# Queries' input loaded by row groups and turned by VectorE in place of TensorE, with each group's first scores ahead of its products, in a prompt-token cross-attention kernel

## Chip, core and metric

The kernel runs on one core of one Trainium2 chip. The metric is the device time of one execution in microseconds (us). The engines are named as in the profile: PE is TensorE (matrix products and transposes), PEld its loading of weights, DVE is VectorE, ACT is ScalarE, POOL is GpSimd, and SP is SyncE, which here only issues DMAs. The time before is 429.61 us, the median of three runs (429.59 to 430.12).

## What is computed

Cross-attention with 20 heads of width 16 over 371 text tokens, plus a second attention over four prompt tokens whose logits get a cosine term. The batch has 8 elements of 112 queries with 320 channels; the context has 375 rows of 512, the last four being the prompt tokens. All is fp32. The reference, cut to what matters:

```python
B, S, C = hidden_states.shape                      # 8, 112, 320
text_ehs, ip_ehs = ehs[:, :-4], ehs[:, -4:]        # 371 and 4 rows of 512
q = heads(hidden_states @ W_q)                     # 20 heads of 16
k_t, v_t = heads(text_ehs @ W_k), heads(text_ehs @ W_v)
probs_t = softmax(einsum('bhsd,bhtd->bhst', q, k_t) * attn_scale)
text_out = einsum('bhst,bhtd->bhsd', probs_t, v_t)
k_ip, v_ip = heads(ip_ehs @ W_k_ip), heads(ip_ehs @ W_v_ip)
qsem = l2norm(einsum('bhst,bte->bhse', probs_t, text_ehs))
sem = einsum('bhse,bne->bhsn', qsem, l2norm(ip_ehs))
fused = einsum('bhsd,bhnd->bhsn', q, k_ip) * attn_scale + 0.5 * sem
probs_ip = softmax(fused) * spatial_mask[None, None, :, None]
out = (text_out + einsum('bhsn,bhnd->bhsd', probs_ip, v_ip)) @ W_out + b_out + x
```

The kernel never forms qsem. Its norm is a quadratic form of the probabilities in the Gram matrix of the context, and its product with the prompt tokens is a product of the probabilities with a small matrix.

## The kernel before

**Steps.** The work runs in 40 steps (b, g): eight batch elements, five groups of four heads each. A step's main work on PE are the *products* (`multiplied`, L748): the turned probabilities times `u`, a matrix that holds the upper blocks of the Gram matrix, the values and the prompt columns. They go over 12 blocks of 32 text tokens, and in each block over the group's four heads, which sit in four 32-row groups of PE and sum in four PSUM banks (pool `ps_qd`, tag "qd", four buffers, one bank for each head). At the step's end ACT copies the values' columns out of each bank (`value_sums`, L761), and DVE multiplies the rest with the probabilities and reduces it (`reduced`, L794, tile `junk`, sum `ss`). After its reduction a bank is free for the next step's products.

**The way from scores to products.** The *scores* (L686, tile `ps_s`, pool `ps_sc`, two buffers) of step n + 2 are made during step n: those of heads 2 and 3 behind the first block of the products, those of heads 0 and 1 behind the seventh. For each, DVE takes the maximum (L709, `nmx`), ACT the exponential (L712, `p`) and copies the four prompt scores (L714, `ipl`), and SP issues a DMA that brings the probabilities into a row-grouped layout (L721, `xg`). After the third block of the products, DVE turns the next step's `xg` into `xgT` (L729, a 32x32 block transpose).

**Work between the steps.** `between(b, g)` issues, behind the products of each step, what the next element needs: the Gram matrix at g = 0 and with it the turn of a later context on DVE (L404), the values at g = 1 and 2 (L578), the keys at g = 2, 3 and 4 (L544; the last third is put together by PE transposes of `k3`, L535), the output of the element before (`finish`: transposes of `attn` into `ps_a`, L950, copied by ACT to `aT`, L954; the output product `ps_o`, L962). These use the pool `ps_mm` (tag "mm", two buffers), or a buffer of the scores' pool where `bank(..., spare=True)` asks for it.

**Queries.** `project_queries` prepares the queries of one or two elements: element 0 in the prologue, the pair (1, 2) over step (0,1) and what follows, (3, 4) from step (1,3) on, (5, 6) from (3,3), 7 from (5,3). PE transposes x in three pieces of 128, 128 and 64 channels (L333, `ps_x`), ACT copies each to `xT` (L336), and three products with W_q (L344, `ps_q`) follow at later places, whose results DVE masks into `qm` (L353). For a pair, the first product stands at g = 4 of the first element, the second and third at g = 3 and 4 of the next.

**Order.** The order on PE, SP and DVE is that of the code, and in the prologue and from the main loop on that of ACT too. Waits come only from the data, the buffers of the pools, and SP's DMA semaphores: there are eight in turn, so that a DMA of SP waits until the eighth before it has landed. All input loads of the prologue go through SP in one row.

Of the kernel before, what the change touches and what calls it, by code (L numbers as in the profile page):

```python
# [20 lines left out]
def kernel(  # L21
# [149 lines left out]
    make_identity(nc, ident)  # L171
    nc.gpsimd.memset(wq_sb[REST:, FULL, :], 0.0)

# [141 lines left out]
    def project_queries(bs):  # L315
        n = len(bs)
        end = bs[0] == B - 1
        xT = work.tile([P, NC, 2 * S], F32, tag="xT", name=f"xT_{bs[0]}", bufs=1)
        qm = work.tile([P, NC, 2, 2 * S], F32, tag="qm", name=f"qm_{bs[0]}", bufs=2)

        qT = const.tile([P, NC, S], F32, tag="qT", name="qT") if bs[0] == 0 else None
        for j, b in enumerate(bs):
            queries[b] = (qT, qm, j)
        nc.gpsimd.memset(xT[REST:, FULL, :], 0.0)
        for i in range(NC):
            cn = min(P, C - i * P)
            if bs[0] == 0:

                ps = ps_qd.tile([P, 512], F32, tag="qd", name=f"ps_x_0_{i}")
            else:  # L330
                ps = bank(f"ps_x_{bs[0]}_{i}", spare=i > 0)
            for j, b in enumerate(bs):
                nc.tensor.transpose(  # L333
                    ps[:cn, j * S : (j + 1) * S], x_sb[:, b, i * P : i * P + cn], ident[:S, :S]
                )
            nc.scalar.copy(xT[:cn, i, : n * S], ps[:cn, : n * S])  # L336
            yield
        for i in range(NC):
# [4 lines left out]
            for j in range(NC):  # L343
                nc.tensor.matmul(  # L344
                    ps[:, : n * S],
                    wq_sb[:, j, i * P : (i + 1) * P],
                    xT[:, j, : n * S],
                    start=(j == 0),
                    stop=(j == NC - 1),
                )  # L350
# [174 lines left out]
    def keys(b):  # L525
# [409 lines left out]
    def prompt_sums_and_projection(b, s, eng, part, n, h0, i0, i1, w, attn, ah):  # L935
# [11 lines left out]

        ps = bank(f"ps_a_{b}_{h0}", spare=True)
        for i in range(i0, i1):
# [129 lines left out]
    def between(b, g):  # L1079
# [16 lines left out]
        if g == 1:  # L1096
            if new:
                run(("v", nb), lambda: values(nb), 1 if b == 0 else 2)
            if b == 0:
                run(("pp",), prompt_projections)  # L1100
            for bs in first if b == 0 else ():
                run(("q", bs[0]), lambda: project_queries(bs), 3)
        if g == 2 and new:
            run(("v", nb), None)
            run(("k", nb), lambda: keys(nb))
            for bs in first if b == 0 else ():
                run(("q", bs[0]), None)
        if g == 2 and b > 0 and new:
            run(("f", b - 1), None, 2)
        if g == 3:  # L1110
            if new:
                run(("k", nb), None, 1)
            if b > 0 and new:
                run(("f", b - 1), None)
            for bs in first if b > 0 else ():
                run(("q", bs[0]), lambda: project_queries(bs), 3)
            if b == 0:
                run(("t", b), lambda: prompt_logits(b))
            for bs in rest:
                run(("q", bs[0]), None)  # L1120
        if g < NT and nb + 1 < B:
            run(("c", nb + 1), lambda: transposed_context(nb + 1))
        if g == 4:
            if b > 0 and new:
                run(("f", b - 1), None, 2)
            if nb < B - 1:
                run(("k", nb), None, 1)
            for bs in (first if b > 0 else []) + (rest if b < B - 2 else []):
                run(("q", bs[0]), None)

    prompts = normalised_prompts()
# [9 lines left out]
    next(context)  # L1141
    order_values()
    drain(products)
    nc.scalar.preload_act_table(AF.Exp)
    gram_to_groups(0, range(QN - 1))
    run(("v", 0), lambda: values(0))
    run(("q", 0), lambda: project_queries(pairs[0]), 3)
    gram_to_groups(0, (QN - 1,), nc.scalar)
# [9 lines left out]
    for a in range(GROUP):  # L1158
        scores(0, 0, a, early=True)
        probabilities(0, 0, a)  # L1160
    drain(transposed_context(1))
    run(("q", 0), None)
    run(("k", 0), None)
    for a in range(GROUP):
        scores(0, 1, a, early=True)
        probabilities(0, 1, a)
    load_embed(nc.sync, wkip_sb, w_k_ip)
    load_embed(nc.sync, wvip_sb, w_v_ip)
# [11 lines left out]
    def load_rest(n):  # L1180

        if n == 0:
            load_x(1, 3)
        elif n == 2:
# [217 lines left out]
```

## Time and profile before

| what | value |
|---|---|
| runs: median (lowest to highest) | 429.61 us (429.59 to 430.12) |
| the profiled execution | 429.75 us |
| its span in the trace | 428.0 us |
| instructions in the trace | 13975 |
| mean granted clock of PE | 0.999 of full |

The span is the time from the first to the last recorded instruction; 1.75 us of the execution lie around it. The timelines give start and duration in us, then the engine, line, operation and tiles; instructions of one kind that follow each other are put together with their count, and in brackets stands an idle time before them with what ended it. A group's row gives its busy time in all, the mean of one in ns, and its idle time before.

### The profile page before, as it was taken

To read this page: it belongs to the slowest core of one execution; us is meant where nothing else is said; L and a number is where in the kernel's file an instruction comes from. 1 tells how busy PE (TensorE), PEld (TensorE's weight loads), DVE (VectorE), ACT (ScalarE), POOL (GpSimd) and SP (SyncE) were. 2 spreads that over 40 slices of the span, in tenths; PEclk is the share of its full clock that TensorE was granted. 3 is DMA by queue.
4 is the path that set the end of the run, shared out by engine and by line. 5 is a ranking of instruction groups with operands and counts; after the bars stand their busy time and mean duration, and the time that the engine had idled before them with its cause. 6 is when DMAs were issued, how large, how long until landed. Compare 5 with 4: busy or idle time off the path is not lost.

```text
span 428.0 us, 13975 instructions
## 1 busy us (share of the span) xinstructions
PE 419.5 (98%) x5521; PEld 330.3 (77%) x5521; DVE 327.8 (77%) x672; ACT 189.7 (44%) x659; POOL 111.1 (26%) x275
## 2 busy tenths in 40 slices
PE   8999999989999999999999999999999999999995
PEld 8867768878777877789777977788777887687993
DVE  5038569787887879788797878887788977889873
ACT  2344342346334353345435363334634363446773
POOL 5310101112060212411152121511133120515550
PEclk9999999999999999999999999999999999999999
DMA  8776665687645956476646956468556536564200
GB/s 239 199 192 211 140 169 157 160 200 149 166 123 138 207 152 179 123 162 150 168 121 160 189 124 170 127 153 175 141 166 153 145 96 173 156 159 121 65 2 27
DMA packets 57630, 64.26 MB, mean 150 GB/s; under 512 B 18448, under 2 KB 51592, under 8 KB 57566
## 3 DMA queue, kind: packets, MB, share of 16 engines
q1 hardware_dynamic: 56934, 62.42, 58.2%
q8 instruction: 43, 0.70, 0.8%
q10 hardware_dynamic: 632, 0.96, 0.7%
q14 instruction: 21, 0.17, 0.1%
HBM read 18.67 MB, written 5.32 MB: 56 GB/s over the span
## 4 chain that ended last, share of the span: by engine, by line
PE 90%; DVE 3%; ACT 3%; DMA 1%; issue 1%; POOL 0%; DVEq 0%; ACTq 0%
PE ps_qd L748 43%; PE ps_v L578 15%; PE ps_k L544 10%; PE ps_g L502 7%; PE ps_s L686 5%; PE ps_q L344 3%; PE ps_o L962 2%; PE ps_g L458 1%; DVE junk L794 1%; ACT shared L787 1%; DMA xg<-p 1%; DVE nmx L709 1%; DMA ct<-in_ctx_dram 1%; PE ps_k L560 1%; PE ps_c L417 1%
## 5 line engine op out<-in xcount | busy, mean ns | idle before, releaser
L748 PE MATMUL ps_qd<-u,xgT 32*112 32x168 f32 (+11 forms) x3840 | 221.7, 353 | 0.3 <-POOL u L655 0.3
L748 PEld LDWEIGHTS ps_qd<-u,xgT 32*112 32x112 f32 x3840 | 189.0, 172 | 33.7 <-issue 10.4
L729 DVE STREAM_TRANSPOSE xgT<-xg 128x1536 f32<-128x1536 f32 (+1 forms) x45 | 119.3, 2672 | 6.7 <-DMA xg<-p 6.7
L712 ACT ACTIVATE p<-ps_s,nmx 112x371 f32<-112x371 f32 x156 | 84.8, 582 | 74.8 <-DVE nmx L709 63.5
L709 DVE TENSOR_REDUCE nmx<-ps_s 112x1 f32<-112x371 f32 x160 | 77.5, 529 | 42.2 <-PE ps_s L686 41.3
L794 DVE CUSTOM_DVE_ANT_0 junk<-ps_qd,p 112x371 f32<-112x371 f32 x146 | 79.2, 542 | 17.4 <-PE ps_qd L748 1.4
L686 PE MATMUL ps_s<-kT,qm 32*112 32x375 f32 (+1 forms) x320 | 65.5, 484 | 0.1
L655 POOL COPY u<-vr 128x64 f32<-128x64 f32 x120 | 25.9, 238 | 152.4 <-PE ps_qd L748 100.9
L578 PE MATMUL ps_v<-wv_sb,ctxT 128*128 128x384 f32 (+1 forms) x192 | 63.6, 480 | 0.0
L578 PEld LDWEIGHTS ps_v<-wv_sb,ctxT 128*128 128x128 f32 x192 | 35.2, 190 | 19.7
L544 PE MATMUL ps_k<-ctxT,wk_sb 128*128 128x371 f32 x136 | 46.3, 483 | 0.2 <-DVE ctxT L425 0.2
L761 ACT COPY pvs<-ps_qd 112x21 f32<-112x21 f32 x151 | 16.3, 190 | 62.3 <-PE ps_qd L748 61.9
L544 PEld LDWEIGHTS ps_k<-ctxT,wk_sb 128*128 128x128 f32 x136 | 24.9, 190 | 15.2 <-POOL ct L138 0.5
L502 PE MATMUL ps_g<-ctxT 128*32 128x375 f32 (+11 forms) x672 | 30.4, 333 | 0.0
L686 PEld LDWEIGHTS ps_s<-kT,qm 32*112 32x112 f32 x320 | 26.7, 170 | 4.8 <-ACT kT L551 2.0
L502 PEld LDWEIGHTS ps_g<-ctxT 128*32 128x32 f32 x672 | 27.7, 110 | 2.0
L714 ACT COPY ipl<-ps_s 112x4 f32<-112x4 f32 x140 | 23.5, 168 | 0.0
L353 DVE TENSOR_SCALAR qm<-ps_q,emask 128x224 f32<-128x224 f32 (+1 forms) x25 | 9.0, 394 | 17.1 <-PE ps_q L344 17.1
L585 ACT COPY vext<-ps_v 128x384 f32<-128x384 f32 (+1 forms) x24 | 11.3, 469 | 22.4 <-PE ps_v L578 22.3
L404 DVE STREAM_TRANSPOSE ctxT<-ct 128x512 f32<-128x512 f32 x18 | 19.9, 1108 | 1.6 <-DMA ct<-in_ctx_dram 1.6
L475 POOL TENSOR_TENSOR ug<-ug,half 128x128 f32<-128x128 f32 (+1 forms) x24 | 10.5, 450 | 31.9 <-ACT ug L474 31.9
L937 POOL TENSOR_TENSOR wv<-vip,w 112x1280 f32<-112x1280 f32 x6 | 14.8, 2466 | 14.2 <-DVE w L877 14.2
(171 smaller groups left out, 323.8 us busy)
## 6 DMA issues: line engine op xcount, KB each, us to landing
xg<-p SPq DMA_DIRECT2D x156, 162.3 KB
u<-ug SPq DMA_DIRECT2D x124, 99.0 KB
ct<-in_ctx_dram SPq DMA_DIRECT2D x24, 176.0 KB
vr<-vd SPq DMA_DIRECT2D x32, 120.0 KB
vip<-vipd SPq DMA_DIRECT2D x6, 560.0 KB
vd<-vext SPq DMA_DIRECT2D x7, 320.0 KB
vd<-vext SPq DMA_DIRECT2D x7, 160.0 KB
out_dram<-ob SPq DMA_DIRECT2D x8, 140.0 KB
```

Of the source, the lines that this page charges most:

```text
L404: nc.vector.transpose(ctxT[:, :, c * P : (c + 1) * P].rearrange("p e (j i) -> p j e i", i=RG), ct[:, some, :].rearrange("p j (k e) -> p j ...
L502: nc.tensor.matmul(ps[c][q * RG : (q + 1) * RG, j * RG - c * P : T - c * P], ctxT[:, e, j * RG : (j + 1) * RG], ctxT[:, e, j * RG : T], st ...
L544: nc.tensor.matmul(ps[:, :TT], wk_sb[:, e, i * P : (i + 1) * P], s["ctxT"][:, e, :TT], start=(e == 0), stop=(e == NE - 1),)
L578: nc.tensor.matmul(ps[:, :w], ctxT[:, e, c * P : (c + 1) * P], wv_sb[:, e, :w], start=(e == 0), stop=(e == NE - 1),)
L655: nc.gpsimd.tensor_copy(v, dealt(b, c, s["vr"][:, c * QN : (c + 1) * QN, g, :]))
L686: nc.tensor.matmul(ps[:S, :w], qm[a * RG : (a + 1) * RG, i, r, j * S : (j + 1) * S], s["kT"][a * RG : (a + 1) * RG, i, :w], start=True, st ...
L709: nc.vector.tensor_reduce(nmx, ps[:S, :TT], AX.X, ALU.max, negate=True)
L712: nc.scalar.activation(s["p", g][:, a, :], ps[:S, :TT], AF.Exp, bias=nmx)
L714: nc.scalar.copy(s["ipl"][:, groups[g][a], :], ps[:S, TT:T])
L729: nc.vector.transpose(xT[:, j : j + n].rearrange("p j (k q) -> p q j k", q=QN), xg[:, :, j * RG : (j + n) * RG].rearrange("p q (j k) -> p ...
L748: nc.tensor.matmul(banks[a][:S, j * RG : UW], xT[a * RG : (a + 1) * RG, j, :S], region(b, c)[a * RG : (a + 1) * RG, q, j * RG - c * P :], ...
L794: nc.vector.tensor_tensor_reduce(out=junk, in0=ps[:S, :TT], in1=s["p", g][:, a, :], scale=1.0, scalar=0.0, op0=ALU.mult, op1=ALU.add, accu ...
```

## The change

x is loaded a second time, into `xr_sb`: the 320 channels in four blocks of 80, each block in 32 partitions that hold 28 queries, and four such groups of queries side by side on the free axis. That takes four DMAs for an element, each with runs of 80 floats. One DVE instruction per element (a 32x32 block transpose, L349 in the new file) turns it straight into `xT`; PE's transposes, ACT's copies and POOL's clearing of `xT` go. The channels come out in another order, so W_q is loaded with its rows in the same order (`load_blocks`, eight DMAs instead of two). The query products read `xT` in four runs of 28 columns.

The other parts: the turns stand in `between` at g = 0 and 1 of element 0 and at g = 2 and 3 of elements 1, 3, 5 (at 5 only g = 2); the loads for them at g = 0 and 2 of these elements and in the prologue. The scores of heads 2 and 3 come ahead of the products instead of behind their first block. At g = 2 the keys come ahead of the values. The last keys of element 1 use a buffer of `ps_mm`, and so do all `ps_a`. The prompt logits of element 0 move from g = 3 to g = 4. The plain load of x for element 0 leaves the prologue.

```diff
+    xr_sb = const.tile([P, 2, QN, NC * RG], F32, tag="xr_sb", name="xr_sb")
+    nc.vector.memset(xr_sb[:, 0], 0.0)
     wq_sb = const.tile([P, NC, CP], F32, tag="wq_sb", name="wq_sb")
+    nc.vector.memset(wq_sb[:, FULL, :], 0.0)
...
+    XB = C // QN
+    XR = XB - 2 * RG
+
+    def load_blocks(eng, t, w):
+
+        for a in range(QN):
+            eng.dma_start(
+                t[a * RG : (a + 1) * RG, :2, :C],
+                w[a * XB : a * XB + 2 * RG, :].rearrange("(e k) f -> k e f", k=RG),
+            )
+        for a in range(QN):
+            eng.dma_start(t[a * RG : a * RG + XR, 2, :C], w[a * XB + 2 * RG : (a + 1) * XB, :])
+
+    def load_x_blocks(b, j):
+
+        for a in range(QN):
+            nc.sync.dma_start(
+                xr_sb[a * RG : a * RG + S // QN, j, :, :XB],
+                x[b, :, a * XB : (a + 1) * XB].rearrange("(q i) f -> i q f", q=QN),
+            )
...
-    nc.sync.dma_start(x_sb[:, 0, :], x[0])
-    load_channels(nc.sync, wq_sb, w_q)
+    load_x_blocks(0, 0)
+    load_blocks(nc.sync, wq_sb, w_q)
     load_embed(nc.sync, wk_sb, w_k)
...
-    nc.gpsimd.memset(wq_sb[REST:, FULL, :], 0.0)
+    nc.gpsimd.memset(xr_sb[:, 1], 0.0)
...
-        xT = work.tile([P, NC, 2 * S], F32, tag="xT", name=f"xT_{bs[0]}", bufs=1)
+        xT = work.tile([P, NC, 2, QN, RG], F32, tag="xT", name=f"xT_{bs[0]}", bufs=1)
...
-        nc.gpsimd.memset(xT[REST:, FULL, :], 0.0)
-        for i in range(NC):
-            cn = min(P, C - i * P)
-            if bs[0] == 0:
-
-                ps = ps_qd.tile([P, 512], F32, tag="qd", name=f"ps_x_0_{i}")
-            else:
-                ps = bank(f"ps_x_{bs[0]}_{i}", spare=i > 0)
-            for j, b in enumerate(bs):
-                nc.tensor.transpose(
-                    ps[:cn, j * S : (j + 1) * S], x_sb[:, b, i * P : i * P + cn], ident[:S, :S]
-                )
-            nc.scalar.copy(xT[:cn, i, : n * S], ps[:cn, : n * S])
+            nc.vector.transpose(
+                xT[:, :, j].rearrange("p e q i -> p q e i"),
+                xr_sb[:, j].rearrange("p q (e k) -> p q e k", k=RG),
+            )
             yield
...
-                    xT[:, j, : n * S],
+                    xT[:, j, :n, :, : S // QN],
...
-            ps = bank(f"ps_k_{b}_{i}", spare=0 < b < B - 1 and i == FULL)
+            ps = bank(f"ps_k_{b}_{i}", spare=1 < b < B - 1 and i == FULL)
...
-        ps = bank(f"ps_a_{b}_{h0}", spare=True)
+        ps = bank(f"ps_a_{b}_{h0}")
...
         if g == 2 and new:
+            run(("k", nb), lambda: keys(nb))
             run(("v", nb), None)
-            run(("k", nb), lambda: keys(nb))
...
-            for bs in first if b > 0 else ():
-                run(("q", bs[0]), lambda: project_queries(bs), 3)
...
+        for bs in first:
+            if g in ((0, 1) if b == 0 else (2, 3)[: len(bs)]):
+                run(("q", bs[0]), lambda: project_queries(bs))
...
+        if g in (0, 2) and b + 2 in (3, 5, 7) and b + 2 + g // 2 < B:
+            load_x_blocks(b + 2 + g // 2, g // 2)
...
         now, more, then = ahead(n)
+        for c, a in now:
+            scores(*c, a)
+            probabilities(*c, a)
         for j, _ in enumerate(multiplied(b, g)):
             if j == 0:
-                for c, a in now:
-                    scores(*c, a)
-                    probabilities(*c, a)
```

Three places show what this does to the order. First PE behind the products of step (1,3): the keys, the output's transposes, and then the next step (1,4). `ps_x` are the transposes of x, `ps_qd_4_0` to `_3` the four banks of the products, `ps_s_1_2` and `ps_s_1_3` scores of heads 2 and 3. Before:

```order
L544 MATMUL ps_k_1_1678<-ctxT_617,wk_sb 128x371 x4
L950 MATMUL ps_a_0_1684<-ident,attn_145 128x112 x3
L333 MATMUL ps_x_0_1693<-ident,x_sb 128x112 x2
L333 MATMUL ps_x_1_1697<-ident,x_sb 128x112 x2
L333 MATMUL ps_x_2_1701<-ident,x_sb 64x112 x2
L748 MATMUL ps_qd_4_0_1705<-u_360,xgT_4_1603 112x392
L748 MATMUL ps_qd_4_1_1706<-u_360,xgT_4_1603 112x392
L748 MATMUL ps_qd_4_2_1707<-u_360,xgT_4_1603 112x392
L748 MATMUL ps_qd_4_3_1708<-u_360,xgT_4_1603 112x392
L686 MATMUL ps_s_1_2_1713<-kT_618,qm_750 112x375
L686 MATMUL ps_s_1_3_1721<-kT_618,qm_750 112x375
```

The same place now:

```order
L560 MATMUL ps_k_1_1689<-ctxT_628,wk_sb 128x371 x4
L966 MATMUL ps_a_0_1695<-ident,attn_157 128x112 x3
L702 MATMUL ps_s_1_2_1702<-kT_629,qm_638 112x375
L702 MATMUL ps_s_1_3_1710<-kT_629,qm_638 112x375
L764 MATMUL ps_qd_4_0_1717<-u_367,xgT_4_1614 112x392
L764 MATMUL ps_qd_4_1_1718<-u_367,xgT_4_1614 112x392
L764 MATMUL ps_qd_4_2_1719<-u_367,xgT_4_1614 112x392
L764 MATMUL ps_qd_4_3_1720<-u_367,xgT_4_1614 112x392
```

The six transposes of x are gone, and the two scores stand ahead of the step's first product instead of behind its fourth. At (2,3) the rows of the keys and of `ps_a` are followed by the second query product, in both kernels:

```order
L560 MATMUL ps_k_1_2373<-ctxT_1304,wk_sb 128x371 x4
L966 MATMUL ps_a_0_2379<-ident,attn_158 128x112 x3
L360 MATMUL ps_q_1_2385<-xT_1579,wq_sb 128x224 x3
L702 MATMUL ps_s_1_2_2391<-kT_1305,qm_1580 112x375
L702 MATMUL ps_s_1_3_2399<-kT_1305,qm_1580 112x375
```

What moved there is the buffer: `ps_k_1` and `ps_a_0` now take the two buffers of `ps_mm` in turn, and `ps_q_1` that of `ps_k_1`; before, `ps_a_0` took one of the scores' pool. The third place is DVE behind the reductions of step (1,2), with the turn of a context (`ctxT`), the maxima for step (1,3)'s scores and the turn of the probabilities for step (1,4). Now:

```order
L420 STREAM_TRANSPOSE ctxT_1304<-ct_1108 128x4x4x32
L349 STREAM_TRANSPOSE xT_1579<-xr_sb 128x4x3x32
L725 TENSOR_REDUCE nmx_0_2_1585<-ps_s_0_2_1583 112x1
L725 TENSOR_REDUCE nmx_0_3_1593<-ps_s_0_3_1591 112x1
L745 STREAM_TRANSPOSE xgT_4_1614<-xg_155 128x4x384
```

The second row is new; before, the maxima (L709) followed the context's turn (L404) directly.

More of the change, by code (lines that the diff above doesn't have):

```diff
@@ L1129, in between @@
                 run(("q", bs[0]), None)
+            if b == 0:
+                run(("t", b), lambda: prompt_logits(b))
     prompts = normalised_prompts()
@@ L1142 @@
     order_values()
+    run(("q", 0), lambda: project_queries(pairs[0]))
     drain(products)
@@ L1146 @@
     run(("v", 0), lambda: values(0))
-    run(("q", 0), lambda: project_queries(pairs[0]), 3)
     gram_to_groups(0, (QN - 1,), nc.scalar)
@@ L1160 @@
         probabilities(0, 0, a)
+    load_x_blocks(1, 0)
     drain(transposed_context(1))
@@ L1166 @@
         probabilities(0, 1, a)
+    load_x_blocks(2, 1)
     load_embed(nc.sync, wkip_sb, w_k_ip)
```

6 lines of the change are left out of this document (1 added, 5 removed).

## Prediction

> **What bounds the kernel now.** I read the page's busy row first, then the granted clock, then the chain of work that ended last.
>
> ```profile
> PE 419.5 (98%) x5521; PEld 330.3 (77%) x5521; DVE 327.8 (77%) x672; ACT 189.7 (44%) x659; POOL 111.1 (26%) x275
> PEclk9999999999999999999999999999999999999999
> PE 90%; DVE 3%; ACT 3%; DMA 1%; issue 1%; POOL 0%; DVEq 0%; ACTq 0%
> ```
>
> PE (TensorE) is busy for 98% of the span at the full granted clock, and nine tenths of the chain is PE. So work taken off PE shortens the kernel by about its own length, unless something else is late at that place. Two engines can be: DVE (77%), which frees the four product banks with its reductions, and ACT (ScalarE, 44%), which frees the others. The profiled execution took 429.75 us (span 428.0); the median of the runs is 429.61, .14 lower. I sum against 429.75.
>
> **Part 1: the transposes that leave PE.** Five groups of queries are prepared: b = 0 in the prologue, then pairs beside step (0,1) and steps (1,3), (3,3), (5,3). From PE's timeline, prologue, (0,1), (1,3) and (5,3):
>
> ```profile
> 16.25 0.45 PE L333 MATMUL ps_x<-ident,x_sb 112*128 112x112 f32 x3
> 16.54 4.49 PE L578 MATMUL ps_v<-wv_sb,ctxT 128*128 128x320 f32 x16
> ...
> 59.89 0.79 PE L333 MATMUL ps_x<-ident,x_sb 112*128 112x112 f32 x6
> 60.62 0.93 PE L748 MATMUL ps_qd<-u,xgT 32*112 32x392 f32 x8
> ...
> 128.70 0.55 PE L333 MATMUL ps_x<-ident,x_sb 112*128 112x112 f32 x4
> 129.47 0.38 PE L333 MATMUL ps_x<-ident,x_sb 112*64 112x112 f32 x2 [0.23 <-ACT aT L954]
> 129.78 1.22 PE L748 MATMUL ps_qd<-u,xgT 32*112 32x392 f32 x10
> 130.55 0.48 PE L686 MATMUL ps_s<-kT,qm 32*112 32x375 f32 x2
> ...
> 326.18 0.35 PE L333 MATMUL ps_x<-ident,x_sb 112*128 112x112 f32 x2
> 327.17 1.22 PE L748 MATMUL ps_qd<-u,xgT 32*112 32x392 f32 x9
> ```
>
> From start to start, PE spends .29 in the prologue (16.25 to 16.54), .73 at (0,1) and 1.08 at (1,3) (128.70 to 129.78, its wait for ACT's aT in it). Step (3,3) has the same instructions as (1,3), so 1.08 too. That is 3.18. At (5,3) .99 stand on PE, but there the chain shows what is late next:
>
> ```profile
> 326.75 3.14 DMA xg<-p
> 329.97 2.14 DVE xgT L729
> ```
>
> The probabilities' turn through a DMA and DVE carries the end there, not PE. PE ahead by .99 gains a part only; I take .4, between 0 and .99.
>
> **Part 2: the stalls that go with them, and the scores moved ahead.** First the one wait that the waits view puts on the copy that is removed, then PE's timeline at (0,2), at the end of (0,4), and at (2,2):
>
> ```profile
> PEld ps_s L686 <- ACT xT L336: 0.7, 1, 0.7
> ```
>
> ```profile
> 61.60 0.79 PE L686 MATMUL ps_s<-kT,qm 32*112 32x371 f32 x2
> ...
> 87.12 0.54 PE L535 MATMUL ps_k<-ident,k 128*128 128x128 f32 x3 [1.08 <-ACT ipl L714]
> 88.74 1.32 PE L748 MATMUL ps_qd<-u,xgT 32*112 32x392 f32 x9
> ...
> 158.97 1.22 PE L748 MATMUL ps_qd<-u,xgT 32*112 32x392 f32 x9
> 159.87 0.63 PE L748 MATMUL ps_qd<-u,xgT 32*112 32x392 f32 x3
> ```
>
> At (0,2) the score starts .98 after the step's first product (60.62 to 61.60), at (1,4) .77 (129.78 to 130.55): .2 lost at least, .7 at most by the wait. I take .5. At (0,4) the keys wait 1.08 for ACT to leave a score bank; the transposes now use another bank, so that wait goes. The products behind them need the fourth product bank, which DVE leaves in its own time, so I count .8, between 0 and 1.08. At (2,2) the tenth product waits for DVE and starts at 159.87, .90 after the first; ten products and the scores behind them normally fill .77, of which the tenth starts at about .48. So .42 goes if scores of about .6 (four, in two pairs) stand ahead and cover it. Nowhere else does the moved score change what PE does: it is the same instruction a place earlier, and it gives DVE its input .77 sooner. Sum of part 2: 1.72.
>
> **Part 3: the turn on DVE.** Eight new transposes of 128x384 (seven of them in steps). The nearest rows are other transposes by the same instruction:
>
> ```profile
> L404 DVE STREAM_TRANSPOSE ctxT<-ct 128x512 f32<-128x512 f32 x18 | 19.9, 1108 | 1.6 <-DMA ct<-in_ctx_dram 1.6
> L729 DVE STREAM_TRANSPOSE xgT<-xg 128x1536 f32<-128x1536 f32 x35 | 104.2, 2978 | 6.7 <-DMA xg<-p 6.7
> ```
>
> (2978 − 1108) / (1536 − 512) = 1.83 ns an element; 1108 − 128 x 1.83 = 874 ns, so .87 us each, 7.0 for eight; between .70 (the slope alone) and 1.11 (no less than for 512). What hides it is DVE's wait for PE's scores, which the waits view totals; DVE's timeline at (1,2) to (1,4) shows where the wait is and where it isn't:
>
> ```profile
> DVE nmx L709 <- PE ps_s L686: 41.3, 35, 3.4
> ```
>
> ```profile
> 120.62 1.11 DVE L404 STREAM_TRANSPOSE ctxT<-ct 128x512 f32<-128x512 f32 x1
> 122.04 0.99 DVE L709 TENSOR_REDUCE nmx<-ps_s 112x1 f32<-112x371 f32 x2 [0.31 <-PE ps_s L686]
> ...
> 128.77 0.55 DVE L794 CUSTOM_DVE_ANT_0 junk<-ps_qd,p 112x371 f32<-112x371 f32 x1
> 131.37 0.99 DVE L709 TENSOR_REDUCE nmx<-ps_s 112x1 f32<-112x371 f32 x2 [2.05 <-PE ps_s L686]
> ```
>
> The turn of g = 3 falls in the 2.05 before 131.37 and is hidden. The turn of g = 2 comes right behind 120.62 and ends at about 122.6, where the maximum started at 122.04: DVE is .5 later for the step, and the fourth bank comes free at about 129.8 instead of 129.3 (128.77 + .55). PE, now at 128.70 where its transposes stood, does its scores (.6) and three products and wants that bank at about 129.5. So some .3 is lost at b = 1 and as much at b = 3; b = 5 has its own term. **.6 off the gain**, between 0 and 1.0.
>
> [...]
>
> **Part 4: a new wait for the queries.** In the changed order the output's transposes (ps_a) take the bank that the second query product used to find free, so that product now takes the bank of the keys just ahead and waits for ACT's copy of them. From PE's and ACT's timelines at (2,3):
>
> ```profile
> 178.03 0.45 PE L950 MATMUL ps_a<-ident,attn 112*128 112x112 f32 x3
> 178.32 1.31 PE L344 MATMUL ps_q<-xT,wq_sb 128*128 128x224 f32 x6
> ```
>
> ```profile
> 178.23 0.47 ACT L551 COPY kT<-ps_k 128x371 f32<-128x371 f32 x1 [1.15 <-PE ps_k L544]
> ```
>
> PE could start the queries at 178.32; ACT is done at 178.23 + .47 = 178.70. That is .4 at each of (2,3), (4,3) and (6,3), with the next step's scores and products queued behind: **1.2 off the gain**, between 0 (if DVE is what the step waits for anyway) and 1.2.
>
> **Part 5: the extra DMAs.** Each load of x by row groups is four DMAs on SP, in the prologue W_q is eight instead of two. From SP's, POOL's, DVE's and PE's timelines of the prologue:
>
> ```profile
> 4.85 1.03 SPq L119 DMA_DIRECT2D wk_sb<-in_L_xattn_W_k_dram  x1
> 9.70 0.29 SPq L155 DMA_DIRECT2D ct<-in_ctx_dram  x1
> 24.92 1.88 SPq L603 DMA_DIRECT2D vr<-vd  x4
> 40.08 5.69 SPq L145 DMA_DIRECT2D ct<-in_ctx_dram  x4
> 45.93 3.55 SPq L721 DMA_DIRECT2D xg<-p  x4
> ```
>
> ```profile
> 16.40 0.40 POOL L1153 COPY wv_sb<-wk_sb 128x256 f32<-128x256 f32 x1
> ```
>
> ```profile
> 52.08 2.97 DVE L729 STREAM_TRANSPOSE xgT<-xg 128x1536 f32<-128x1536 f32 x1
> ```
>
> ```profile
> 21.54 2.76 PE L544 MATMUL ps_k<-ctxT,wk_sb 128*128 128x371 f32 x8
> ```
>
> In the program each of SP's DMAs waits for the eighth before it to have landed. The last ct piece at 9.70 is the eighth after wv_in; now the fourth W_q block is, so it goes at 9.70, four more of .47 (1.88 / 4, pieces of the same run length) follow, and W_k leaves at about 11.9 instead of 4.85. Its transfer takes between 3.1 (the xg row above) and 11.6 (4.85 to its first reader at 16.40), so it lands between 15 and 23.5; PE needs it at 21.25. I take nothing, with up to 2.2 in the range. Later, eight more pieces (3.8 us of SP) stand ahead of the third context's pieces and the xg of 45.93; the first four fall where SP waits for probabilities anyway, the other 1.9 push xg and with it DVE's turn at 52.08. DVE's reductions then end about 60.2, where PE without its transposes wants the first bank at 59.9: **.3 off**, between 0 and 1.0.
>
> The other edits have one answer: keys ahead of values at g = 2, the bank of k at b = 1 (its price is in the .8), prompt_logits at g = 4 and the two DVE memsets at the start are the same work in places where ACT, POOL and SP have over 20% idle; nothing, within .3 either way. Were ACT late, the price would be one copy, .47.
>
> **The sum:** −3.18 − .40 − 1.72 + .6 + 1.2 + .3 = −3.2, so 429.75 − 3.2 = **426.5**. Chance .50.
>
> **The rivals.**
> - **All stalls go** (.16): DVE is .77 earlier from the scores ahead, ACT frees the keys' bank before PE comes. The three costs (2.1) vanish, (5,3) gains its .99, (0,4) its 1.08: 423.5. For it speaks the 41.3 of DVE's waiting; against it that at 122.04 only .31 of it is left.
> - **The gain is given back** (.11): the query products read xT in four runs of 28 columns instead of one row. No row shows such an operand. Their group is
>
> ```profile
> L344 PE MATMUL ps_q<-xT,wq_sb 128*128 128x224 f32 (+1 forms) x90 | 16.8, 323 | 0.1
> ```
>
> if each costs a sixth more, 2.8 of 16.8 come back: 429.3. Nothing in the rows speaks for or against the size; the same columns are read in number.
> - **Slower: the turn isn't hidden** (.10). DVE sets the pace of the odd batches: each of the eight turns then delays the banks by its .87, 7.0 in place of my .6, 432.9. It decides where the fourth bank (129.8) is later than PE by more than what DVE's next wait for scores gives back; 2.05 at 131.37 speaks against it.
> - **Slower: the small loads are slow** (.06). If each of the twelve pieces of x and W_q cost SP what the ct pieces at 40.08 did (5.69 / 4 = 1.42), W_k would be issued at 3.3 + 12 x 1.42 = 20.3 and land, by 3.1 to 11.6, at 23.4 to 31.9: 2 to 10 late, at 6.8 (near the middle) 5.9: 432.4. [...]
> - **Prologue late by 1 to 2** (.07): W_k at the long end of part 5: 428.
>
> **How the numbers follow.** Range 422.5 to 430.0: down to the lower ends of parts 3 to 5 with a little over, up to the case that gives the gain back. About .2% (.86 us) is what a measurement of this kernel can tell from no change. Faster by more: the forecast .50, all stalls .16, the late prologue .07 and .01 of the gain given back, .74; within: .10; slower: .16.
>
> **What would show it.** No transposes or copies of x on PE and ACT; PE's start at (1,4) about 1 us earlier relative to the keys ahead; the wait of ps_qd for DVE's sums at (1,4) and (3,4) near .3; the second query product waiting for ACT's kT by about .4 three times; the new transposes at .87; W_k's first reader before 21. I am wrong if DVE's wait for scores falls by much more than 7 us with PE's wait for DVE rising, if the query products' mean rises, or if PE's first keys start after 22.

## The result, and the profile after

The changed kernel takes 428.32 us (median of 20 runs, 426.54 to 430.84); the kernel before took 429.74 beside it (median of 20, 429.03 to 431.05). The ratio is 0.997, with a 95% interval of 0.9956 to 0.9984: faster, by 1.4 us as the medians stand (.7 to 1.9 by the interval). The forecast was 3.2. The direction held and the time lies in the range, but less than half of the gain came. The profiled execution took 428.22 us at a span of 426.2, so it stands close to the median; 1.53 less than the profiled one of before.

The page's busy row and the chain's engines, after:

```profile
PE 416.0 (98%) x5497; PEld 325.1 (76%) x5497; DVE 331.8 (78%) x682; ACT 185.6 (44%) x644; POOL 109.4 (26%) x270
PE 86%; DMA 4%; DVE 4%; ACT 3%; issue 1%; SPq 1%; ACTq 0%; POOL 0%; DVEq 0%
```

PE has 3.5 us less to do (416.0 against 419.5), which is the transposes that left. The span fell by half of that, and the chain has a new part: DMA went from 1% to 4%. To see where, I take the start of the last product of a step in both timelines:

| last product of step | before, us | after, us | difference |
|---|---|---|---|
| (0,0) | 42.24 | 44.40 | +2.17 |
| (1,0) | 94.62 | 95.85 | +1.23 |
| (1,4) | 134.96 | 135.18 | +.22 |
| (2,2) | 164.60 | 164.21 | −.39 |
| (3,4) | 233.90 | 232.81 | −1.09 |
| (4,4) | 283.21 | 282.72 | −.49 |
| (6,4) | 381.82 | 380.63 | −1.19 |
| of the kernel | 414.51 | 412.68 | −1.83 |

From the end of (0,0) on, the changed kernel gains 4.0 us (2.17 + 1.83), more than forecast. **It loses 2.2 us before its first step has ended.** PE's timeline of the prologue after, at the place of the first query product:

```profile
13.93 6.63 PE L594 MATMUL ps_v<-wv_sb,ctxT 128*128 128x320 f32 x24
22.10 0.92 PE L360 MATMUL ps_q<-xT,wq_sb 128*128 128x112 f32 x6 [1.53 <-ACT vext L601]
```

Before, the same product:

```profile
20.86 0.82 PE L344 MATMUL ps_q<-xT,wq_sb 128*128 128x112 f32 x6
```

In brackets: PE stood idle for 1.53 us until ACT had copied the values out of a bank; the product starts 1.24 later than before. ACT's timeline at that time says why ACT was late; "ACTq" rows are DMAs that ACT issues itself:

```profile
16.29 0.43 ACT L601 COPY vext<-ps_v 128x320 f32<-128x320 f32 x1 [0.59 <-PE ps_v L594]
16.36 5.22 ACTq L536 DMA_DIRECT2D u<-ug  x4
21.62 0.75 ACT L601 COPY vext<-ps_v 128x320 f32<-128x320 f32 x2 [4.90 <-DMA u<-ug]
```

Between two copies ACT issues four DMAs of `u`, and they take 5.22 us. In the kernel before, the same four:

```profile
16.81 0.59 ACTq L520 DMA_DIRECT2D u<-ug  x1
...
17.44 1.89 ACTq L520 DMA_DIRECT2D u<-ug  x3
```

They were done in 2.5 us (16.81 to 19.33). ACT's copies stand behind them: the fourth issue ends at 21.58, and the next copy starts at 21.62. What the four wait for is the rotation of eight semaphores. SP does not have it to itself, as the description of the kernel before has it: ACT's DMAs take their turns in the same row. In the trace the second of the four takes the semaphore of W_k's load, which lands at 18.13, and goes at 18.15; the third takes that of a piece of the second context, which lands at 20.40, and goes at 20.42; the fourth takes that of another piece, landed at 20.11, and follows the third at 20.97. SP's timeline of the prologue, after:

```profile
2.83 0.36 SPq L144 DMA_DIRECT2D wv_in<-in_L_xattn_W_v_dram  x1
3.23 1.76 SPq L134 DMA_DIRECT2D xr_sb<-in_x_dram  x4
5.09 4.48 SPq L124 DMA_DIRECT2D wq_sb<-in_L_xattn_W_q_dram  x4
9.69 1.74 SPq L129 DMA_DIRECT2D wq_sb<-in_L_xattn_W_q_dram  x4
11.48 0.69 SPq L144 DMA_DIRECT2D wk_sb<-in_L_xattn_W_k_dram  x1
12.22 1.75 SPq L178 DMA_DIRECT2D ct<-in_ctx_dram  x3
14.01 0.33 SPq L180 DMA_DIRECT2D ct<-in_ctx_dram  x1
14.93 12.63 SPq L536 DMA_DIRECT2D u<-ug  x12
```

W_q's first four pieces take 4.48 because one of them waits 2.8 for `wv_in` to land. W_k goes out at 11.48 (before: 4.85) and the second context at 12.22 (before: 5.92). The table of windows, from 7 to 13 and from 13 to 19 us, shows what the DMA engines make of it; the last two numbers are their busy share and GB/s. Before:

```profile
7.00:13.00 6.00, 6.00 (x51) 5.84 (x51) 2.74 (x7) 1.03 (x2) 0.66 (x4) 1.00 1.05 322
13.00:19.00 6.00, 6.00 (x33) 4.61 (x32) 0.00 (x0) 2.80 (x7) 3.80 (x14) 1.00 0.46 112
```

After:

```profile
7.00:13.00 6.00, 6.00 (x52) 5.84 (x51) 3.01 (x8) 1.03 (x2) 0.52 (x5) 1.00 0.40 100
13.00:19.00 6.00, 6.00 (x29) 4.55 (x29) 0.00 (x0) 2.36 (x4) 2.82 (x11) 1.00 0.93 271
```

The DMA engines are more than half idle while SP waits and issues small pieces (.40 busy from 7 to 13 us), and busy (.93 from 13 to 19) just when the u DMAs want slots that the late loads hold.

The other .94 of the 2.17 comes at the first products. SP's own u DMAs are late in the same row (the last is issued by 27.56, before 23.30), and behind them the DMAs of the first probabilities (29.85, before 26.97). The products start when DVE has turned these, at 39.15:

```profile
29.85 3.72 SPq L737 DMA_DIRECT2D xg<-p  x4
36.21 2.94 DVE L745 STREAM_TRANSPOSE xgT<-xg 128x1536 f32<-128x1536 f32 x1 [1.20 <-DMA xg<-p]
```

In the steps, most of what was forecast is there. PE's timeline at (1,3) and (1,4), after:

```profile
127.03 2.76 PE L560 MATMUL ps_k<-ctxT,wk_sb 128*128 128x371 f32 x8
129.63 0.45 PE L966 MATMUL ps_a<-ident,attn 112*128 112x112 f32 x3
130.01 0.57 PE L702 MATMUL ps_s<-kT,qm 32*112 32x375 f32 x2
130.02 0.58 PE L764 MATMUL ps_qd<-u,xgT 32*112 32x392 f32 x2
```

From the keys' start to the first product PE needs 2.99 (127.03 to 130.02); before it was 3.97 (125.81 to 129.78):

```profile
125.81 2.76 PE L544 MATMUL ps_k<-ctxT,wk_sb 128*128 128x371 f32 x8
```

The products of heads 0 and 1 start beside the scores of heads 2 and 3, in other row groups (130.02 and 130.01). New waits of PE stand at (0,3), behind (0,4) and behind (2,3):

```profile
72.84 0.57 PE L702 MATMUL ps_s<-kT,qm 32*112 32x375 f32 x2 [0.64 <-DVE qm L369]
89.87 0.76 PE L681 MATMUL ps_ip<-kipb,qT 128*112 128x32 f32 x6 [0.80 <-ACT kT L556]
178.35 1.40 PE L360 MATMUL ps_q<-xT,wq_sb 128*128 128x224 f32 x6 [0.27 <-ACT kT L567]
```

The last is the second query product. With it the stretch from the end of (2,3) to the end of (2,4) is .52 longer than before, and so it is at (4,4) and (6,4).

The turns and the query products, as groups:

```profile
L349 DVE STREAM_TRANSPOSE xT<-xr_sb 128x384 f32<-128x384 f32 x8 | 4.4, 552 | 0.0
L360 PE MATMUL ps_q<-xT,wq_sb 128*128 128x224 f32 (+1 forms) x90 | 17.1, 326 | 2.3 <-ACT vext L601 1.5
```

A turn takes .55, not .87, and reading `xT` in four runs changes next to nothing (326 ns against 323). DVE waits for other things than before; the waits view after:

```profile
DVE nmx L725 <- PE ps_s L702: 12.2, 10, 3.4
DVE xgT L745 <- DMA xg<-p: 12.8, 7, 2.6
```

DVE waited 41.3 us for scores and waits 12.2 now, but its wait for the probabilities' DMA rose from 6.7 to 12.8, and others with it. In all it stood idle for 100.2 us of the span before and for 94.4 now, so its slack shrank by little more than the 4.4 of the turns.

### The profile page after: what moved, and what is told of

It is laid out like the page before. It is cut to its first block, busy times and chain, and to the rows that moved or that the text cites. A ratio compares the mean times of both kernels' runs of the same rounds, so it can differ in the third digit from the quotient of the medians.

```text
span 426.2 us, 14007 instructions
## 1 busy us (share of the span) xinstructions
PE 416.0 (98%) x5497; PEld 325.1 (76%) x5497; DVE 331.8 (78%) x682; ACT 185.6 (44%) x644; POOL 109.4 (26%) x270
## 4 chain that ended last, share of the span: by engine, by line
PE 86%; DMA 4%; DVE 4%; ACT 3%; issue 1%; SPq 1%; ACTq 0%; POOL 0%; DVEq 0%
PE ps_qd L764 38%; PE ps_v L594 13%; PE ps_k L560 10%; PE ps_s L702 10%; PE ps_g L518 7%; PE ps_q L360 3%; PE ps_o L978 3%; DMA ct<-in_ctx_dram 2%; DMA wv_in<-in_L_xattn_W_v_dram 2%; DVE junk L810 1%; DVE nmx L725 1%; ACT shared L803 1%; PE ps_k L576 1%; PE ps_ipkv L304 1%; DMA xg<-p 0%
## 5 line engine op out<-in xcount | busy, mean ns | idle before, releaser
L745 DVE STREAM_TRANSPOSE xgT<-xg 128x1536 f32<-128x1536 f32 (+1 forms) x45 | 119.3, 2670 | 23.3 <-DMA xg<-p 12.8
L725 DVE TENSOR_REDUCE nmx<-ps_s 112x1 f32<-112x371 f32 x160 | 76.8, 524 | 13.5 <-PE ps_s L702 12.2
L702 PEld LDWEIGHTS ps_s<-kT,qm 32*112 32x112 f32 x320 | 22.9, 170 | 12.6 <-issue 10.8
L601 ACT COPY vext<-ps_v 128x384 f32<-128x384 f32 (+1 forms) x24 | 11.2, 471 | 34.0 <-PE ps_v L594 29.1
L420 DVE STREAM_TRANSPOSE ctxT<-ct 128x512 f32<-128x512 f32 x18 | 20.0, 1114 | 4.1 <-DMA ct<-in_ctx_dram 4.0
L360 PE MATMUL ps_q<-xT,wq_sb 128*128 128x224 f32 (+1 forms) x90 | 17.1, 326 | 2.3 <-ACT vext L601 1.5
```

Source lines behind the costliest of these rows:

```text
L360: nc.tensor.matmul(ps[:, : n * S], wq_sb[:, j, i * P : (i + 1) * P], xT[:, j, :n, :, : S // QN], start=(j == 0), stop=(j == NC - 1),)
L702: nc.tensor.matmul(ps[:S, :w], qm[a * RG : (a + 1) * RG, i, r, j * S : (j + 1) * S], s["kT"][a * RG : (a + 1) * RG, i, :w], start=True, st ...
L725: nc.vector.tensor_reduce(nmx, ps[:S, :TT], AX.X, ALU.max, negate=True)
L745: nc.vector.transpose(xT[:, j : j + n].rearrange("p j (k q) -> p q j k", q=QN), xg[:, :, j * RG : (j + n) * RG].rearrange("p q (j k) -> p ...
```

## The experiments

My theory after the result: the prologue's loads cost some 2 us, through the order of SP's rotation; the steps gain what was forecast or more. Rivals: DVE, late by its turns, gives the gain back in the steps; or the moved scores push the products back. Ratios are against the kernel before, run beside each; the changed kernel's is 0.997. Where I compare single executions, I count from the end of (0,0), since the prologue varies from run to run: with the same loads it ended between 42.38 and 44.48 in six profiles. Some steps vary as well. In five profiles whose steps are those of the kernel before, (2,2) takes 10.72 to 11.45 us, (5,4) 9.50 to 10.49 and (6,0) 8.75 to 9.60; in three with the steps of the changed kernel they take 10.72 to 11.69, 8.69 to 9.53 and 8.29 to 9.19. In the latter (0,2), (2,0) and (4,0) vary by .4 to .5 as well. The steps (1,4), (2,4), (3,4) and (4,4) agree within .04 in each set, so a difference of two single profiles can be trusted there, and not in the steps that vary.

**W_k ahead of W_q's pieces** (changed kernel):

```diff
-    load_blocks(nc.sync, wq_sb, w_q)
     load_embed(nc.sync, wk_sb, w_k)
+    load_blocks(nc.sync, wq_sb, w_q)
```

> The changed kernel with W_k's load ahead of the eight pieces of W_q. Theory (the loss is in the prologue: the pieces push W_k's issue from 4.85 to 11.48, its transfer meets the u DMAs, ACT's four u issues stretch from 2.5 to 5.2 us, its value copies and the first query product come late): W_k is issued by 6, ACT's four issues take about 2.5 again, the first query product starts within .3 us of the values' end, and the time is 1.5 to 2.2 us below the changed kernel, about 3.3 below the kernel before. Rival A (the loss lies in the main loop, DVE being late by its turns): no change from the changed kernel, about 1.4 below before. Rival B (ACT is late because it now issues its four u DMAs without the copies of x between them): W_k early, the wait of the first query product stays at 1.5.

Ratio 0.9972 (0.9949 to 0.9994): no change from the changed kernel, a miss for the theory in this form. W_k did go out at 5.35, but the context pieces only at 13.4, and the u DMAs still waited. In its profile (0,0) ends at 43.52, .88 earlier:

```profile
10.33 3.05 SPq L129 DMA_DIRECT2D wq_sb<-in_L_xattn_W_q_dram  x4
13.42 2.04 SPq L178 DMA_DIRECT2D ct<-in_ctx_dram  x3
```

```profile
16.15 4.65 ACTq L536 DMA_DIRECT2D u<-ug  x4
```

So W_k's issue alone is not the matter; now the second context's pieces come late in the rotation. The next run moves them too.

**W_k and the second context ahead of W_q's pieces** (changed kernel):

```diff
-    load_blocks(nc.sync, wq_sb, w_q)
     load_embed(nc.sync, wk_sb, w_k)
     loaded[1] = load_ctx(1)
+    load_blocks(nc.sync, wq_sb, w_q)
```

> The changed kernel with W_k and the second context loaded ahead of the eight pieces of W_q. With W_k alone ahead the u DMAs still waited, for the context pieces that went out at 13.4. Theory (the u DMAs and ACT's value copies wait for the last loads in the rotation, whichever they are): the context pieces go out by 11, the DMA share from 7 to 13 us is over .8, ACT's four u issues take 2.5 to 3.5, the products of (0,0) end by 42.7 (44.40 in the changed kernel), and the time is 1 to 1.7 us below the changed kernel's. Rival (the pieces of W_q themselves are slow and now late): the spread of W_q on POOL and the first query product wait for them, no gain.

Ratio 0.9916 (0.9891 to 0.9941), median 426.83: the gain against before is 3.6 us instead of 1.4. The end of (0,0) is at 41.47 in its profile, 2.93 earlier than in the changed kernel's; from there on the two differ by .2. This profile is of the fastest of its six executions (424.85); by the ratios the order is worth 2.3 us, and the intervals of the two kernels don't meet. Windows and ACT's issues:

```profile
7.00:13.00 6.00, 5.51 (x47) 5.50 (x48) 2.88 (x8) 1.09 (x3) 0.79 (x5) 1.00 1.09 291
13.00:19.00 6.00, 6.00 (x28) 4.44 (x27) 0.00 (x0) 2.45 (x5) 2.50 (x10) 1.00 0.48 121
```

```profile
16.06 2.74 ACTq L536 DMA_DIRECT2D u<-ug  x4
```

ACT's four issues are short again with no copies of x between them, so rival B of the run before falls. And W_q's eight pieces do no harm as the last in the row: in the three orders run with these loads, ACT's u DMAs are late where the second context's large loads stand behind the pieces (3.22 to 5.22 us for the four issues in four profiles, 2.54 and 2.74 in the two with the loads ahead).

**The kernel before with only its loads cut.** x for element 0 in four pieces and W_q in eight, all in whole rows of 1280 bytes:

```diff
-    nc.sync.dma_start(x_sb[:, 0, :], x[0])
-    load_channels(nc.sync, wq_sb, w_q)
+    for a in range(QN):
+        r = slice(a * S // QN, (a + 1) * S // QN)
+        nc.sync.dma_start(x_sb[r, 0, :], x[0, r, :])
+    for a in range(QN):
+        r = slice(a * RG, (a + 1) * RG)
+        nc.sync.dma_start(
+            wq_sb[r, :FULL, :C], w_q[: FULL * P, :].rearrange("(i p) f -> p i f", p=P)[r]
+        )
+    for a in range(QN):
+        r = slice(a * REST // QN, (a + 1) * REST // QN)
+        nc.sync.dma_start(wq_sb[r, FULL, :C], w_q[FULL * P + r.start : FULL * P + r.stop, :])
```

> The kernel before, whose load of x for element 0 is cut into four pieces of 28 rows and whose load of W_q is cut into eight pieces, as many as in the changed kernel but with whole rows of 1280 bytes; nothing else is changed. Theory (the number of pieces in SP's rotation of eight semaphores makes W_k and the context pieces late, and with them ACT's u DMAs and value copies): the DMA share from 7 to 13 us falls from 1.05 to about .5, the products of (0,0) end 1 to 2.2 us later, and the time is 1 to 2.2 us above before. Rival (the 320-byte runs are what is slow): the prologue as before, within .4 us.

Ratio 1.006 (1.0035 to 1.0084), median 433.45: twelve pieces in this order cost 1.5 to 3.6 us, without a 320-byte run. Its windows are those of the changed kernel:

```profile
7.00:13.00 6.00, 5.34 (x46) 5.26 (x46) 2.63 (x7) 1.02 (x2) 0.79 (x5) 1.00 0.44 111
```

Its profiled execution, though, was its fastest (429.81) and shows only .3 at the end of (0,0). Three more runs follow: one with W_q's pieces at the end (the order of the run above, in this kernel), and two more profiles of the same kernel.

> The kernel before with x's and W_q's loads cut into twelve whole-row pieces, as in the run that was 1.006 of before, but with W_k and the second context loaded ahead of W_q's eight pieces. Theory (the order in the rotation is all of it): within .6 us of before, the DMA share from 7 to 13 us about 1. Rival (twelve pieces cost time wherever they stand): 2 to 3 us above before again.

Ratio 1.0004 (0.9989 to 1.0019): the loss is gone with the order, at the same number of pieces. From 7 to 13 us:

```profile
7.00:13.00 6.00, 5.27 (x45) 5.26 (x46) 2.64 (x7) 1.02 (x2) 0.79 (x5) 1.00 1.06 296
```

> A second look at the kernel before with the cut loads in the old order: its profiled execution was its fastest, 429.81, at a median of 433.45. Theory: an execution near the median shows the loss at the end of (0,0), 1.5 to 3 us later than before's 42.24, with ACT's four u issues stretched to 4 or more. Rival: (0,0) ends within .5 of before's and the loss lies in the steps.

> A third look at the same kernel, with the same expectations: by the theory the end of (0,0) and the time move together, a us for a us; by the rival they don't.

The first of the two took 431.98 and ended (0,0) at 43.87, 1.64 late, with ACT's last three u issues only at 20.15 (17.44 before):

```profile
20.15 1.84 ACTq L529 DMA_DIRECT2D u<-ug  x3
```

The second took 431.32 and ended (0,0) at 42.41, .17 late: its loss is not in the prologue. It lost .35 in the steps and 1.0 behind the last product: from DVE's last result to the end of the trace, while SP stores that result, 4.1 us pass instead of 3.0. No trace ties this to the loads. So the end of (0,0) and the time don't move together a us for a us. Both times also lie in the range of before's runs beside them (428.95 to 432.21). That the order of the loads removes the loss is shown by the timed runs (1.006 and 1.0004, whose intervals don't meet). Where the 3 us of the first one's median lie is not settled: one profile in three shows 1.6 us in the prologue.

**The scores behind the first block again** (changed kernel):

```diff
-        for c, a in now:
-            scores(*c, a)
-            probabilities(*c, a)
         for j, _ in enumerate(multiplied(b, g)):
             if j == 0:
+                for c, a in now:
+                    scores(*c, a)
+                    probabilities(*c, a)
```

> The changed kernel with the scores of heads 2 and 3 behind the first block of the products again. Theory (scores and products of different row groups overlap, so the place costs PE nothing, and ahead they save waits for banks): .3 to 1.0 us slower than the changed kernel, with waits of the products for DVE's sums back at (2,2) and at g = 0. Rival (scores ahead push the products back by their own length, .3 to .6 in each of 34 steps where a bank is late): faster than the changed kernel by 1 us or more.

Ratio 1.0065 (1.0031 to 1.0098), median 433.63. The sign is the theory's, the size isn't: about 4 us (1.0065 less .997) where I had written at most 1. The rival falls. In the waits view PE's weight loads for products wait longer for DVE's sums, here and in the changed kernel:

```profile
PEld ps_qd L764 <- DVE ss L810: 4.8, 12, 0.5
```

```profile
PEld ps_qd L764 <- DVE ss L810: 1.8, 5, 0.4
```

DVE and PE at (1,4) show one such wait:

```profile
131.14 0.57 DVE L349 STREAM_TRANSPOSE xT<-xr_sb 128x384 f32<-128x384 f32 x1
132.26 1.13 DVE L725 TENSOR_REDUCE nmx<-ps_s 112x1 f32<-112x371 f32 x2 [0.55 <-PE ps_s L702]
```

```profile
130.66 1.22 PE L764 MATMUL ps_qd<-u,xgT 32*112 32x392 f32 x9
131.42 0.47 PE L702 MATMUL ps_s<-kT,qm 32*112 32x375 f32 x1
131.70 0.49 PE L764 MATMUL ps_qd<-u,xgT 32*112 32x392 f32 x3
```

The tenth product waits for its bank until 131.70, and the score behind it, for which DVE waits in turn, is late too; against the changed kernel's profile eleven steps are .3 to 1.0 longer. As I read it, PE and DVE wait for each other there, and the scores ahead break that circle; no run tests this reading.

**The kernel before with only the scores ahead** (the same edit, the other way):

> The kernel before with only the scores of heads 2 and 3 moved ahead of the products. Undone in the changed kernel, this move cost over 5 us, since the products' banks came late by then. Theory (ahead, the scores let DVE finish its reductions earlier; before, banks are late at g = 0, (0,2), (1,0), (2,2), (5,4) and (6,0) by some 2 to 3 us in all): 1.5 to 2.5 us below before. Rival (the move only repairs what DVE's new turns break): within .5 us of before.

Ratio 1.0061 (1.0038 to 1.0084), median 432.77: slower by 2.6 us. Both expectations fall. (Their "over 5 us" compares medians; the ratios give about 4.) The bank waits did go, but there is a new one, as PE at (1,3) and the waits view show:

```profile
118.20 2.66 PE L544 MATMUL ps_k<-ctxT,wk_sb 128*128 128x371 f32 x8
121.41 0.57 PE L686 MATMUL ps_s<-kT,qm 32*112 32x375 f32 x2 [0.56 <-ACT kT L551]
```

```profile
PE ps_s L686 <- ACT kT L551: 3.3, 6, 0.6
PEld ps_s L686 <- ACT xT L336: 2.1, 4, 1.2
```

The first scores of an element read keys that PE has only just made, and ACT must copy them first. So the score's place goes with the order of keys and values, and in this kernel with ACT's copies of x, for which the scores wait 2.1 us. The next run takes the first apart.

**Values ahead of keys at g = 2 again** (changed kernel; the two `run` lines in the old order):

> The changed kernel with the values ahead of the keys at g = 2 again. The kernel before with only the scores moved ahead was 1.006 of before: its scores at (n,3) waited .6 to .7 for ACT's copy of keys that PE had just made. Theory (the scores can stand ahead only because the keys are made 2.8 us earlier): at steps (0,3) to (5,3) the scores wait .5 to .7 for ACT's kT, 3.5 to 4.3 us above the changed kernel. Rival (that wait was made by ACT's copies of x, which are gone): within .5 of the changed kernel.

Ratio 1.005 (1.003 to 1.007), median 432.45, 3.4 us above the changed kernel by the ratios (1.005 less .997 of 430). In the profile each of (1,3) to (5,3) is .72 later and (6,3) .63. It is the same wait as in the run before, though ACT's copies of x are gone; the rival falls.

```profile
PE ps_s L702 <- ACT kT L567: 3.3, 6, 0.6
```

**The output's transposes in the scores' pool again** (changed kernel; `bank(..., spare=True)` for `ps_a`):

> The changed kernel with the output's transposes in a buffer of the scores' pool again. Theory: the second query product's three waits for ACT's kT (.52 each) go, 1.5 us, but the scores that now stand right behind wait for ACT's copy aT, .5 to .7 at steps (1,3), (3,3), (5,3) and .2 at the other three: within .7 of the changed kernel either way. Rival (the scores have a buffer in time): 1.5 us below the changed kernel.

Ratio 0.9971 (0.9948 to 0.9995), as the theory has it: in the profile the three waits of the query product go (.52 each), and (1,3), (3,3), (5,3) lose .77, .77 and .88.

**The second query product ahead of the output's transposes** (changed kernel):

```diff
+            for bs in rest:
+                run(("q", bs[0]), None)
             if b > 0 and new:
                 run(("f", b - 1), None)
-            for bs in rest:
-                run(("q", bs[0]), None)
```

> The changed kernel with the second query product ahead of the output's transposes at g = 3. Theory: the query product takes the free buffer, and the transposes the keys' buffer .65 us later, when ACT has copied it: the three waits of .52 go, 1.5 us below the changed kernel, about 2.9 below before. Rival (the steps behind wait for DVE anyway): within .4 of the changed kernel, the wait reappearing at the next products.

Ratio 0.9948 (0.9922 to 0.9974): .9 us below the changed kernel by the ratios, with intervals that overlap, so timing alone does not show the gain. In the profile (2,3), (4,3) and (6,3) gain .53, .53 and .34; the rest of the 1.5 is not there.

**Each turn twice** (changed kernel; a second `nc.vector.transpose` of the same block into a tile that nobody reads):

> The changed kernel with each of the eight turns of x done a second time on DVE, into a tile that nobody reads: .55 us of DVE work eight times more, 4.4 in all. Theory (DVE has .3 to .6 left at the steps of the turns): products wait .2 to .4 at (1,4), (3,4) and (0,2), .5 to 1.5 us above the changed kernel. Rival A (the turns aren't hidden at all): 3.5 to 4.4 above. Rival B (wholly hidden): within .3.

Ratio 0.9995 (0.9975 to 1.0016): about 1.1 us above the changed kernel for 4.4 us of DVE work. Rival A falls. The interval overlaps the changed kernel's, so how much of the 1.1 is real, and with it the choice between the theory and rival B, stays open. In the profile (0,1) and (1,1) take .49 and .33 more and (4,0) .58, while (1,0) takes .53 less. Even by the far ends of the two intervals (1.0016 less .9956) no more than 2.6 of the 4.4 us show. The turns as they stand leave the waits of PE's weight loads for DVE's sums at 1.8 us (1.6 before).

**The best version.** Loads with W_q last and the second query product first:

> The order of loads of the run before this, and at g = 3 the second query product ahead of the output's transposes. Theory: both gains add, 2.4 to 3.2 us below the changed kernel, 3.8 to 4.6 below before. Rival (the loads bring nothing): 1.4 to 1.6 below the changed kernel.

Ratio 0.9889 (0.986 to 0.9917), median 424.99 against 430.37: by the ratio 4.8 us below before and 3.5 below the changed kernel, faster than both. What it gains over the run with the loads alone (1.2) lies within the intervals. With the prompt logits of element 0 at g = 3 as well:

> W_k and the second context loaded ahead of W_q, the second query product ahead of the output's transposes, and element 0's prompt logits at g = 3 behind that query product, so that they no longer wait .8 for ACT's copy of the last keys. Theory: .4 to .8 below the run with the first two parts, 4.5 to 6 below before. Rival (the .8 returns as a wait for a product bank at (1,0)): as that run, within .3.

Ratio 0.99 (0.9877 to 0.9923), median 425.21: nothing more, as the rival has it. The profile is of its slowest execution (428.21), so only the place of the logits is read from it. In the run with two parts the step behind the logits had shrunk already (from the end of (0,4) to the next product 2.92, 3.39 in the changed kernel), and the logits now lengthen g = 3 by the .5 that they take (4.03 to 4.54), while g = 4 stays at 2.98.

## Why the prediction was right or wrong

- **The step that failed is part 5's "I take nothing"**, for W_k's late issue. The issue time was right (11.9 forecast, 11.48), and so was W_k's own reader: W_k lands at 18.13, and it isn't what PE waits for. But I priced only that reader. What became late were the DMAs that reuse the slots of W_k and of the context pieces behind it, and ACT, which issues four of them in order ahead of two copies for which PE waits. By the same row the first step's products wait for their probabilities' turn (the scores stand at 38.30, the products at 39.25). The prologue came out at +2.17 instead of −.29, which is 2.5 us. The steps gained 1.1 more than forecast (4.0 against 2.9), and .3 lies outside the recorded instructions; together that is the miss of 1.7 between the two profiled executions. The 2.17 is one profile and near the upper end: with these loads the prologue ended .1 to 2.2 later than before in six. The timed run needs no profile: with W_k and the context ahead of W_q the gain is 3.6, .4 above the forecast.
- **A sign that I had named** came true: PE's first keys start at 22.86, after the 22 of the prediction. Of the other sign only half came: DVE's wait for scores fell by 29.1, but PE's wait for DVE's sums stayed (1.6 and 1.8). The rival "prologue late by 1 to 2" named the place, and its 428 is close to the 428.32 measured, but by W_k landing late for PE, which didn't happen (18.13, where PE first reads it at 22.86); that the number fits is luck. Its chance of .07 was far too low for a thing whose range I had put at 0 to 2.2.
- **Part 1** held: 1.0 each at (1,3) and (3,3) against 1.08, .72 at (0,1) against .73. (5,3) to (6,0) gained .92 against .4 (.8 to 1.7 over the profiles).
- **Part 2** gained .46 at (2,2) against .42, but the agreement is luck: in two of five profiles with before's steps the tenth product isn't late there at all (10.72 us), and in one with the changed kernel's steps (2,2) takes 11.69. Nor does the trace of before show .48 for the tenth product: at (1,4) the tenth starts .76 behind the first (129.78 to 130.54). From the end of (0,1) to the end of (1,0) it fell short: with part 1's .73 and less part 5's .3 I had 1.7 there, and .94 came. At (0,3) the scores wait .64 for `qm` from DVE, and the moved prompt logits wait .80 for ACT's last keys. That nowhere else the moved score changes what PE does was wrong: alone, in the kernel before, the move costs 2.6 us. It needs the keys' move, which I put at nothing, within .3 either way; without that the changed kernel is 3.4 slower. As both edits were made, neither error shows by itself in the time.
- **Part 3** was too dear: .55 a turn instead of .87, and no bank late at (1,4). Step (4,0) takes 8.80 to 9.18 in three profiles against 8.82 to 8.85 before, so of the .6 at most .4 shows. The slope between the shapes of two other turns was the wrong row to scale by: the measured .552 is 1.44 ns per element, where those two take 2.16 and 1.94.
- **Part 4** held in its mechanism, the wait of the query product on ACT's kT: .52 three times against .4, 1.6 in all where I had put at most 1.2.
- **The rivals.** Only x's pieces have runs of 320 bytes; W_q's have rows of 1280 in both kernels, which part 5 overlooked. SP's four pieces of x took 1.76 us to issue, .44 each where the rival of the small loads has 1.42; four whole-row pieces took 1.69, and the cut loads without such runs lost as much. No run here shows that the runs' size costs the kernel time. That the turns aren't hidden is ruled out by the run with each turn twice, and the query products' four runs of columns cost 3 ns each, .3 us in all.

## What to carry to other kernels

When a load is cut into more DMAs and the program's DMAs share a rotation of semaphores, count the whole row behind it, up to the last DMA that reuses a slot, and look at which engines issue DMAs in order ahead of work that others wait for; pricing the load's own reader is not enough. Here it helped to put the few large loads ahead of the many small pieces, although the pieces' own reader comes first (the first query product at 20.10, the second context's first transpose at 24.94, with W_q last). A reordering can be worth 4 us in company and cost 2.6 alone, so price the parts of a change together, at the place where one makes room for the other.

## What was not expected of the hardware

Products of two row groups run beside scores of the other two: the step from (1,1) to (1,2) takes 10.72 us with the two scores behind the first block and with them ahead. A turn's time does not follow one line in the number of elements: 552 ns for 384, 1114 for 512, 1599 for 768, 2976 for 1536. The first reads and writes runs of 32 elements side by side; the second reads every fourth element, and the last two write every fourth. That this is the reason was not tried.
